# State-space scan on tiles of 32 channels by 4 states: factors in PSUM, both products on GpSimd

## The chip, the core and the metric

The kernel runs on one core of a Trainium2 chip. A core has five engines that run their own instruction streams in order and meet only through semaphores: TensorE (PE, matmuls), VectorE (DVE), ScalarE (ACT), GpSimd (POOL) and SyncE (SP), which here issues all DMAs. Data lies in SBUF (128 partitions), in PSUM (eight banks, into which PE writes; DVE and ACT reach it too), or in memory outside the core.

The metric is the time of one execution on the device in microseconds (us). Durations of single instructions are in nanoseconds (ns) where marked so.

## What is computed

Eight batches of 512 tokens with 256 channels pass through attention, an FFN whose operands are quantised to four bits, a Mamba block that works in both directions, and the FFN again. The change is in Mamba's scan. In one direction it reads, cut to what matters:

```python
def _ssm_dir(xs, conv_w, conv_b, xproj_w, dt_w, dt_b, A_log, D_skip):
    xc = jax.nn.silu(_causal_depthwise_conv(xs, conv_w, conv_b))
    x_dbl = xc @ xproj_w
    dt, B_ssm, C_ssm = jnp.split(x_dbl, [DT_RANK, DT_RANK + D_STATE], axis=-1)
    dt = jax.nn.softplus(dt @ dt_w + dt_b)
    A = -jnp.exp(A_log)
    dA = jnp.exp(dt[..., None] * A)
    dBu = dt[..., None] * B_ssm[:, :, None, :] * xc[..., None]
    def step(h, inp):
        dAt, dBut, ct = inp
        h = dAt * h + dBut
        y = jnp.einsum('bdn,bn->bd', h, ct)
        return (h, y)
    ...
    return y + xc * D_skip
```

There are 512 inner channels (d) and 16 states (n), so each batch and direction has 8192 recurrences over 512 tokens. For every one of them the kernel needs a decay factor exp(dt * A), a first product (dt * xc) * B, the recurrence, and a second product with C; the 16 states of a channel are then summed.

## The kernel before

**Streams.** The program is written as generators that are advanced in turns (`interleave`, `run`, L885 to L955): `thread_a` is attention of a batch, `thread_b` holds merge and second FFN of a finished batch, Mamba's front of the next and the first FFN of the one after, and `thread_s` is the scan. The loop at L953 runs the scan of batch b beside attention of b + 3 and the other work. A planner then orders the instructions of each engine before the run, with the scan at the lower priority (OS = 0 against OA = OB = 1000). The order that each engine gets is fixed in the program.

**Preparation of a scan.** `ssm_prep` (L773) does half of the channels (256) of one direction at a time: it computes dt (softplus written out: Relu, Abs, Exp and Ln on ACT, two sums on POOL at L811 and L813, two steps on DVE at L812 and L815), and u = dt * xc on POOL (L816). Both stay in SBUF with two channel blocks side by side, 128 partitions by 2 x 512. B and C of all states go to memory (bcd).

**Scan.** `ssm` (L819) has channels on the partitions. One round treats one state of 256 channels: SP loads B and C of that state, spread over all partitions (rep, L825); ACT writes the factors (abuf, L829; two instructions of 512, since A is a scalar of each partition); DVE makes the first product (L830) and the scan (L834) over both blocks at once, with an empty column between them where h starts again at zero; POOL makes the second product (L835); PE transposes the tiles onto one PSUM bank for each block, adding up the 16 states (L838). After 16 rounds ACT copies the sums (L844), PE turns them back (L848 through L127), and DVE adds xc * D (L852). There are 32 such passes of 16 rounds: 512 in all. All four operands of scan and products lie in SBUF; there is one factor buffer (NA = 1) and three of h (NH4 = 3).

**Other work that the text speaks of.** `roped` and `latents` (L374, L397) make attention's rotated latents: DVE multiplies out of PSUM (L384), POOL adds (L386) and takes the low parts (L403). `fp4` (L490) quantises: a product on POOL (L506), three steps on DVE (L507 to L509), a product on POOL (L510), with small DVE steps ahead of them (L498 to L503). `newton_rsqrt` (L267) is a chain of tiny DVE steps (L273 to L275). `conv` (L685) has DVE's L693 and L695 with all operands in SBUF; `mamba_pre` has L733. `mm` (L92) is the helper under whose line (L98) most matmuls stand. PSUM banks are named at L86: pa and po for attention, pb for FFN and merge, pp for Mamba's front and preparation, y0 and y1 for the scan's sums.

Of the kernel before, what the change touches and what calls it, by code (L numbers as in the profile page):

```python
# [35 lines left out]
def shape_constants():  # L36
    """Tables and masks that depend on shapes alone, side by side in one array."""
# [16 lines left out]
    parts = [("cos", cos), ("sin", sin), ("m8", mask8), ("m4", mask4), ("id", ident), ("up", up), ("lo", lo), ("rot", rot)]  # L54
# [8 lines left out]
def tile_hybrid(ctx: ExitStack, tc: tile.TileContext, w: dict, consts: bass.AP, out: bass.AP):  # L63
# [11 lines left out]
    PB, TB, HB, QB, QA, HT = 2, 3, 3, 3, 2, 1  # L75
    LAG, TC, XB, YT = 2, 4, 3, 2
    NH4, NA, NU, NDT, TA, RB = 3, 1, 3, 2, 2, 4
# [8 lines left out]
    BANKS = {"pa": 2, "po": 1, "pb": 2, "pp": 1, "y0": 1, "y1": 1}  # L86
# [13 lines left out]
    # ---------------------------------------------------------------- constants  # L100
# [11 lines left out]
    m8, m4, ident = cview("m8"), cview("m4"), cview("id")  # L112
# [16 lines left out]
    def split_rows(dst, row, n):  # L129
        """row [1, n] on partition 0 -> dst [2, n] float32r with the high and the low part."""  # L130
        hl = work([1, 2, 512], FPR, "rep", RB)
        S.copy(hl[:, 0, :n], row)
        V.tensor_tensor(hl[:, 1, :n], row, hl[:, 0, :n].bitcast(F32), ALU.subtract)
        nc.sync.dma_start(dst[0:1, :n].bitcast(F32), hl[:, 0, :n].bitcast(F32))
        nc.sync.dma_start(dst[1:2, :n].bitcast(F32), hl[:, 1, :n].bitcast(F32))

    # ------------------------------------------------------- attention weights
# [15 lines left out]
    def prep_attention():  # L153
        caw = []
        for k in range(3):
            caw.append(work([P, 2, C], F32, "u", NU))
            nc.sync.dma_start(caw[k], w["c_attn_w"][2 * k * P : (2 * k + 2) * P, :].rearrange("(a p) c -> p a c", p=P))
# [84 lines left out]
        # cproj, transposed, and the vector that every bias behind the softmax adds up to  # L242
# [23 lines left out]
    # ------------------------------------------------------------- layer norm  # L266
    def newton_rsqrt(dst, v, n, th):  # L267
        """dst = v ** -0.5 by Newton's iteration; v becomes -v / 2."""
# [8 lines left out]
    def stats(src, th, twice=False):  # L277
        """Means of the rows of src [P, NT, C] and the reciprocal square roots of variance + eps; with twice, behind
        these what two layer norms in a row scale by: the second acts on variance / (variance + eps)."""
# [28 lines left out]
    def token_transpose(dst, src, tag="pb"):  # L308
        """src [P, NT, C] tokens on partitions -> dst [P, 2, T] channels on partitions."""
# [6 lines left out]
    # -------------------------------------------------------------- attention  # L316
    def attention_front(b):
        """The normalised rows, transposed, and the latents of the first four heads."""
# [55 lines left out]
    def roped(xT, g, q):  # L374
        """Rotated latents of four heads [latent, token]; q: 0 for queries, 1 for keys."""
# [13 lines left out]
    def spill(hl, order):  # L389
        """hl [(head, latent), high/low, token] -> memory [part, latent, head, token] with the parts in order."""  # L390
# [6 lines left out]
    def latents(xT, g):  # L397
        """High and low parts of the keys and of the queries of four heads, in memory."""
# [18 lines left out]
    # (head of a pair, number of tiles before the last one) whose scores share a bank  # L417
    PACKS = [[(0, 3)], [(1, 3)], [(0, 2), (0, 0)], [(1, 2), (1, 0)], [(0, 1), (1, 1)]]

    def heads(g, lat, y):  # L420
        qst = [work([98, 2, T], FPR, f"qst{pr}", 1) for pr in range(2)]
        for pr in range(2):
# [3 lines left out]
            # row maxima, negated  # L426
# [62 lines left out]
    # -------------------------------------------------------------------- FFN  # L489
    def fp4(dst, src, n, tag, twice=False, pp=P):  # L490
        """Block-wise FP4 quantise and dequantise of src [pp, n] along the free dim into dst. A multiple of the step
        (half of the power of two below the value, at least 0.5) is what is left when 1.5 * 2**23 steps have been added
        and taken away again; or-ing 22 << 23 into an exponent of 128 or 129 adds 22 to it, and leaves a smaller one
        below 149."""
# [53 lines left out]
    def ffn_front(src):  # L548
        """The normalised and quantised rows, transposed."""
# [52 lines left out]
    def ffns(jobs):  # L602
        """One FFN after the other, as one stream of row tiles; the rows of the next are made ready meanwhile."""
# [26 lines left out]
    # ------------------------------------------------------------------ Mamba  # L630
# [4 lines left out]
    Aneg = const([P, 2, ND, NS], F32, "Aneg")  # L635
# [4 lines left out]
    abuf = [const([P, 2, T + 1], F32, f"abuf{i}") for i in range(NA)]  # L640
    hbuf = [const([P, 2, T + 1], F32, f"hbuf{i}") for i in range(NH4)]
    for t in abuf + hbuf:
        G.memset(t, 0.0)
# [6 lines left out]
    def prep_mamba():  # L650
# [4 lines left out]
        win = [work([P, 2 * INNER], F32, "dt", NDT) for _ in range(2)]  # L655
# [15 lines left out]
        for d, sx in enumerate(("", "_b")):  # L671
            wxp = work([P, 2, T], F32, "tmpA", TA).rearrange("p a t -> p (a t)")[:, : ND * 96].rearrange("p (m n) -> p m n", m=ND)
# [4 lines left out]
            nc.sync.dma_start(Aneg[:, d], w["A_log" + sx].rearrange("(a p) n -> p a n", p=P))  # L677
# [19 lines left out]
    def mamba_pre(src, scr):  # L697
# [13 lines left out]
        token_transpose(xT, xn, "pp")  # L711
        yield
        for m in range(8):
            wp = work([P, 2, P], F32, "xrf", XB)
            nc.sync.dma_start(wp, win_d[m])
            o = psum("pp")
# [56 lines left out]
    def ssm_prep(b, d, c, scr):  # L773
        """Step sizes of half the channels in one direction and their products with the input; B and C in memory."""
        sx = ("", "_b")[d]
        if c == 0:
            us = []
            for i in range(2):
                us.append(work([P, 2, T], F32, "u", NU))
                nc.sync.dma_start(us[i], scr["xc"][4 * d + 2 * i : 4 * d + 2 * i + 2].rearrange("m p t -> p m t"))  # L780
            wxp = work([P, 2, T], F32, "tmpA", TA).rearrange("p a t -> p (a t)")[:, : ND * 96].rearrange("p (m n) -> p m n", m=ND)
            nc.sync.dma_start(wxp, wxp_d[d])
            o = psum("pp")
            for m in range(ND):
                mm(o[:96, :], wxp[:, m, :], us[m // 2][:, m % 2, :], start=(m == 0), stop=(m == ND - 1))
# [4 lines left out]
            fronts[(b, d)] = us, bcd  # L790
            yield
        us, bcd = fronts[(b, d)]
        u = us[c]
        wdt = work([DTR + 1, 2 * P], F32, "wdt", 1)
        cs = slice(2 * c * P, (2 * c + 2) * P)
        nc.sync.dma_start(wdt[:DTR, :], w["dt_w" + sx][:, cs])
        nc.sync.dma_start(wdt[DTR : DTR + 1, :], w["dt_b" + sx][cs].rearrange("(o n) -> o n", o=1))
        dt = work([P, 2, T], F32, "dt", NDT)
        prep[(b, d, c)] = dt, u, bcd
        ex = work([P, 2, T], F32, "tmpA", TA)  # L800
        for e in range(2):
            o = psum("pp")
            PE.matmul(o, wdt[:, e * P : (e + 1) * P], dbt[: DTR + 1, :], start=True, stop=True)
            S.activation(dt[:, e, :], o, AF.Relu)
            S.activation(ex[:, e, :], o, AF.Abs)
            yield
        S.activation(ex, ex, AF.Exp, scale=-1.0)
        lg = work([P, 2, T], F32, "tmpA", TA)
# [7 lines left out]
        G.tensor_tensor(u, dt, u, ALU.mult)  # L816
        yield

    def ssm(b, d, scr):  # L819
        for c in range(2):  # L820
            dt, u, bcd = prep.pop((b, d, c))
            yps = [psum(f"y{i}") for i in range(2)]
            for n in range(NS):
                bcr = work([P, 2, T], F32, "rep", RB)
                nc.sync.dma_start(bcr, bcd[n][None].to_broadcast([P, 2, T]))  # L825
                seq[0] += 1
                a, h = abuf[seq[0] % NA], hbuf[seq[0] % NH4]
                for m in range(2):
                    S.activation(a[:, m, 1:], dt[:, m, :], AF.Exp, scale=Aneg[:, d, 2 * c + m, n : n + 1])  # L829
                V.tensor_tensor(h[:, :, 1:], u, bcr[:, 0, None, :].to_broadcast([P, 2, T]), ALU.mult)  # L830
                aflat, hflat = a.rearrange("p m t -> p (m t)"), h.rearrange("p m t -> p (m t)")
                if d == 1:
                    aflat, hflat = aflat[:, ::-1], hflat[:, ::-1]
                V.tensor_tensor_scan(hflat, aflat, hflat, 0.0, ALU.mult, ALU.add)  # L834
                G.tensor_tensor(h[:, :, 1:], h[:, :, 1:], bcr[:, 1, None, :].to_broadcast([P, 2, T]), ALU.mult)  # L835
                for m in range(2):
                    for i in range(NT):
                        PE.matmul(yps[m][:, i * P : (i + 1) * P], h[:, m, 1 + i * P : 1 + (i + 1) * P], ident,  # L838
                                  start=(n == 0 and i == 0), stop=(n == NS - 1 and i == NT - 1), is_transpose=True)
                yield  # L840
            yts = []
            for i in range(2):
                yts.append(work([P, T], F32, "yt", YT))
                S.copy(yts[i], yps[i])  # L844
            for i in range(2):
                o = psum("pp")
                for q in range(NT):
                    transpose(o[:, q * P : (q + 1) * P], yts[i][:, q * P : (q + 1) * P])  # L848
                xp = work([P, T], F32, "xp", 1)
                m = 2 * c + i  # L850
# [53 lines left out]
    def preps():  # L904
        for b in range(B):
            for d in range(2):
                for c in range(2):
                    yield lambda b=b, d=d, c=c: ssm_prep(b, d, c, scrs[b])
# [79 lines left out]
```

## Time and profile before

| | value |
|---|---|
| time, median of 3 runs | 4627.51 us (4624.49 to 4628.98) |
| the profiled execution: its span from first to last instruction | 4625.4 us |
| PE busy | 3244.4 us, 70% of the span, 12904 matmuls |
| DVE busy | 4028.7 us, 87% |
| ACT busy | 1592.1 us, 34% |
| POOL busy | 2201.7 us, 48% |
| DMA | 628.44 MB, 41.9% of the time of 16 DMA engines |
| TensorE clock granted, mean | 0.804 |

The profile gives the span alone; the median of the runs is 2.1 us above it.

A row of a group reads: line, engine, operation, tile written <- tiles read, shapes, count | busy us in total, mean ns of one | idle us of the engine just before, and what ended most of that. A row of one line's spread has minimum, median and maximum of the duration in ns after the count, then first and last start. A row of the timeline has start and duration in us, and in brackets the idle time before it and what ended it. A row of the windows gives, for a stretch of the span, busy us of PE, weight loads, DVE, ACT and POOL with instruction counts, then the granted clock, the DMA share and GB/s. An instruction that has been issued and cannot proceed counts as busy: its row gets longer.

### The profile page before, as it was taken

What the parts mean: (1) busy time and instruction counts of PE and PEld (TensorE: products, weight loads), DVE (VectorE), ACT (ScalarE), POOL (GpSimd) and SP (SyncE); (2) the same over time, 40 slices, a digit from 0 to 9 for tenths busy, and PEclk for the clock granted to TensorE, in tenths of its full rate; (3) what the DMA queues carried; (4) which work ended last, traced back from release to release, by engine and by line L of the source; (5) the groups of instructions that cost most, each with busy time, mean ns of one, the idle gap of its engine ahead of it and who ended that gap; (6) DMA issues with size and microseconds to landing.
All of it is one profiled execution on the core that took longest, in us unless ns stands there. A gap on an engine that the chain in (4) does not pass through costs nothing. (4 is left out here: it accounts for less than half of the span.)

```text
span 4625.4 us, 40263 instructions
## 1 busy us (share of the span) xinstructions
PE 3244.4 (70%) x12904; PEld 2000.0 (43%) x12904; DVE 4028.7 (87%) x4087; ACT 1592.1 (34%) x2725; POOL 2201.7 (48%) x929
## 2 busy tenths in 40 slices
PE   4879777787776678777777777768745566466456
PEld 2334344344444345444544444445533344345344
DVE  5235599897999996999989998999999999999983
ACT  1223432543443333333343333433433324332320
POOL 3011365445445653545444564565455554555551
PEclk8779878888887799888888888878866777677678
DMA  5223433444454344543454344533543244425232
GB/s 138 85 82 103 141 133 115 152 145 147 159 188 138 115 130 156 166 148 121 153 180 156 119 139 159 185 114 119 167 140 125 100 130 162 147 100 189 98 103 88
DMA packets 349922, 628.44 MB, mean 136 GB/s; under 512 B 50029, under 2 KB 195726, under 8 KB 349710
## 3 DMA queue, kind: packets, MB, share of 16 engines
q1 hardware_dynamic: 349710, 625.85, 41.9%
q8 instruction: 103, 1.69, 0.2%
q14 instruction: 109, 0.89, 0.1%
HBM read 506.85 MB, written 118.88 MB: 135 GB/s over the span
## 5 line engine op out<-in xcount | busy, mean ns | idle before, releaser
L835 POOL TENSOR_TENSOR hbuf<-hbuf,rep 128x1024 f32<-128x1024 f32 x512 | 1304.8, 2549 | 1505.4 <-DVE hbuf L834 688.3
L834 DVE TENSOR_TENSOR_SCAN hbuf<-abuf,hbuf 128x1026 f32<-128x1026 f32 x512 | 1357.7, 2652 | 32.8 <-ACT abuf L829 30.7
L829 ACT ACTIVATE abuf<-dt,Aneg 128x512 f32<-128x512 f32 x1024 | 684.9, 716 | 1699.9 <-DVE hbuf L834 1688.0
L830 DVE TENSOR_TENSOR hbuf<-u,rep 128x1024 f32<-128x1024 f32 x512 | 911.6, 1786 | 37.0 <-issue 19.6
L838 PE MATMUL y<-cst,hbuf 128*128 128x128 f32 x4096 | 690.5, 322 | 355.2 <-POOL hbuf L835 346.7
L838 PEld LDWEIGHTS y<-cst,hbuf 128*128 128x128 f32 x4096 | 579.1, 169 | 517.8 <-POOL hbuf L835 422.9
L98 PE MATMUL pb<-wgu,fxT 128*128 128x352 f32 x1024 | 427.9, 555 | 167.8 <-DVE hff L573 55.5
L433 PE MATMUL pa<-kst,qst 96*128 96x512 f32 (+3 forms) x512 | 229.9, 497 | 237.3 <-DVE tmp L384 100.9
L474 PE MATMUL po<-pt,vs 128*32 128x512 f32 (+3 forms) x1024 | 343.5, 481 | 4.3 <-ACT pt L469 4.2
L98 PEld LDWEIGHTS pb<-wgu,fxT 128*128 128x128 f32 x1024 | 211.5, 223 | 311.3 <-DVE hff L573 75.8
L98 PE MATMUL pa<-xT,wp 128*128 128x512 f32 x512 | 288.1, 694 | 50.4 <-DVE mx L443 29.3
L386 POOL TENSOR_TENSOR tmp<-tmp,tmp 128x512 f32<-128x512 f32 x64 | 124.4, 1944 | 405.8 <-DVE tmp L384 247.6
L98 PE MATMUL pb<-qv,hff 128*128 128x256 f32 x1024 | 261.4, 402 | 38.5 <-DMA qv<-sy 36.0
L98 PE MATMUL pb<-wdn,hT 128*128 128x256 f32 (+1 forms) x768 | 238.9, 455 | 34.5 <-ACT hT L588 14.6
L469 ACT ACTIVATE pt<-pa 128x512 f32<-128x512 f32 x320 | 186.0, 591 | 197.4 <-PE pa L466 135.5
L433 PEld LDWEIGHTS pa<-kst,qst 96*128 96x128 f32 x512 | 120.0, 235 | 305.3 <-DVE tmp L384 123.6
L443 DVE TENSOR_REDUCE mx<-pa 128x1 f32<-128x512 f32 (+2 forms) x384 | 179.0, 497 | 82.7 <-PE pa L435 82.4
L693 DVE SCALAR_TENSOR_TENSOR tmpB<-xs,cw,tmpB 128x512 f32<-128x512 f32 x192 | 243.0, 1265 | 7.6 <-ACT tmpB L691 6.1
L464 PE MATMUL pa<-qst,kst 98*128 98x512 f32 (+3 forms) x512 | 213.5, 464 | 50.4 <-ACT pt L469 23.3
L98 PEld LDWEIGHTS pb<-qv,hff 128*128 128x128 f32 x1024 | 197.3, 201 | 86.0 <-DMA hff<-in_merge_w 22.9
L98 PEld LDWEIGHTS pb<-wdn,hT 128*128 128x128 f32 (+1 forms) x768 | 161.1, 225 | 93.2 <-issue 25.8
L510 POOL TENSOR_TENSOR hff<-qv,qns 128x704 f32<-128x704 f32 x66 | 143.7, 2177 | 104.7 <-DVE qv L509 79.0
(207 smaller groups left out, 4899.3 us busy)
## 6 DMA issues: line engine op xcount, KB each, us to landing
rep<-bcd SPq DMA_DIRECT2D x512, 512.0 KB
hld<-hl SPq DMA_DIRECT2D x192, 256.0 KB
hff<-in_merge_w SPq DMA_DIRECT2D x128, 256.0 KB
qv<-sy SPq DMA_DIRECT2D x128, 256.0 KB
kst<-hld SPq DMA_DIRECT2D x64, 384.0 KB
qst<-hld SPq DMA_DIRECT2D x64, 384.0 KB
wp<-wqk_d SPq DMA_DIRECT2D x64, 256.0 KB
sxc<-tmpB SPq DMA_DIRECT2D x64, 256.0 KB
```

Of the source, the lines that this page charges most:

```text
L98: PE.matmul(o, L, R, start=start, stop=stop, **kw)
L433: PE.matmul(o[:, at : at + n], qst[pr][:96, j, i * P : (i + 1) * P], kst[:96, j, :n], start=(k == 0), stop=False)
L443: V.tensor_reduce(M[:, j, i : i + 1], o[:, at : at + n], AX.X, ALU.max, negate=True)
L464: PE.matmul(o[:, at : at + n], kst[:, j, kt * P : (kt + 1) * P], qst[pr][:, j, kt * P :], start=(k == 0), stop=False)
L469: S.activation(pt, o, AF.Exp)
L474: PE.matmul(po[c : c + 32, kt * P :], vs[:, kt, h * VW : h * VW + 32], pt[:, at : at + n], start=(kt == 0), stop=(kt == 2), tile_position= ...
L693: V.scalar_tensor_tensor(acc, tap(k), cw[:, d, m, k : k + 1], acc, ALU.mult, ALU.add)
L829: S.activation(a[:, m, 1:], dt[:, m, :], AF.Exp, scale=Aneg[:, d, 2 * c + m, n : n + 1])
L830: V.tensor_tensor(h[:, :, 1:], u, bcr[:, 0, None, :].to_broadcast([P, 2, T]), ALU.mult)
L834: V.tensor_tensor_scan(hflat, aflat, hflat, 0.0, ALU.mult, ALU.add)
L835: G.tensor_tensor(h[:, :, 1:], h[:, :, 1:], bcr[:, 1, None, :].to_broadcast([P, 2, T]), ALU.mult)
L838: PE.matmul(yps[m][:, i * P : (i + 1) * P], h[:, m, 1 + i * P : 1 + (i + 1) * P], ident, start=(n == 0 and i == 0), stop=(n == NS - 1 and ...
```

## The change

Channels and states share the partitions: a tile holds 32 channels (q counts four such blocks of 128) times 4 states (g counts four such groups), over 512 tokens. dt and u of a block of 128 channels now go to memory (dud) and come back, each of the four q with its 32 rows repeated for four states; B and C of four states are loaded once for a direction and kept. The factors go to PSUM banks (a), the first product moves from DVE to POOL, and the scan and the second product take a tile of 512. The four tiles of a group are summed over states by four matmuls with a 0/1 matrix (sel, 128 x 32), each into its own 32 columns of PE and its own 32 partitions of one PSUM bank (y); the first of them is made to wait for the group's last product. Transposes, their copies on ACT and the turning back are gone.

```diff
-    PB, TB, HB, QB, QA, HT = 2, 3, 3, 3, 2, 1
-    LAG, TC, XB, YT = 2, 4, 3, 2
-    NH4, NA, NU, NDT, TA, RB = 3, 1, 3, 2, 2, 4
+    PB, TB, HB, QB, QA, HT = 2, 3, 3, 2, 1, 1
+    LAG, TC, XB = 2, 3, 3
+    NHB, NDU, NU, NDT, TA, RB = 8, 5, 4, 2, 3, 5
...
-    BANKS = {"pa": 2, "po": 1, "pb": 2, "pp": 1, "y0": 1, "y1": 1}
+    BANKS = {"pa": 2, "po": 1, "pb": 2, "a": 2, "y": 1}
...
+    sel = (p[:, None] % 32 == np.arange(32)[None, :]).astype(np.float32)
...
-    def ssm_prep(b, d, c, scr):
+    def ssm_prep(b, d, m, scr):
...
         V.tensor_tensor(dt, dt, ex, ALU.add)
         G.tensor_tensor(u, dt, u, ALU.mult)
+        dud = dr.tile([P, 2, T], F32, tag="dud", name=f"dud_{b}_{d}_{m}", bufs=8)
+        prep[(b, d, m)] = dud, fronts[(b, d)]
+        nc.sync.dma_start(dud[:, 0, :], dt)
+        nc.sync.dma_start(dud[:, 1, :], u)
         yield
...
     def ssm(b, d, scr):
-        for c in range(2):
-            dt, u, bcd = prep.pop((b, d, c))
-            yps = [psum(f"y{i}") for i in range(2)]
-            for n in range(NS):
-                bcr = work([P, 2, T], F32, "rep", RB)
-                nc.sync.dma_start(bcr, bcd[n][None].to_broadcast([P, 2, T]))
-                seq[0] += 1
-                a, h = abuf[seq[0] % NA], hbuf[seq[0] % NH4]
-                for m in range(2):
-                    S.activation(a[:, m, 1:], dt[:, m, :], AF.Exp, scale=Aneg[:, d, 2 * c + m, n : n + 1])
-                V.tensor_tensor(h[:, :, 1:], u, bcr[:, 0, None, :].to_broadcast([P, 2, T]), ALU.mult)
...
-                V.tensor_tensor_scan(hflat, aflat, hflat, 0.0, ALU.mult, ALU.add)
-                G.tensor_tensor(h[:, :, 1:], h[:, :, 1:], bcr[:, 1, None, :].to_broadcast([P, 2, T]), ALU.mult)
-                for m in range(2):
-                    for i in range(NT):
-                        PE.matmul(yps[m][:, i * P : (i + 1) * P], h[:, m, 1 + i * P : 1 + (i + 1) * P], ident,
-                                  start=(n == 0 and i == 0), stop=(n == NS - 1 and i == NT - 1), is_transpose=True)
...
+        bcs = None
+        for m in range(ND):
+            dud, bcd = prep.pop((b, d, m))
+            if bcs is None:
+                bcs = []
+                for g in range(4):
+                    bc = work([P, 2, T], F32, "rep", RB)
+                    src = bcd.rearrange("(j g) k t -> g j k t", g=4)[g]
+                    nc.sync.dma_start(bc, src[:, None].to_broadcast([4, 32, 2, T]))
+                    bcs.append(bc)
+            dus = []
+            for q in range(4):
+                du = work([P, 2, T], F32, "du", NDU)
+                nc.sync.dma_start(du, dud[32 * q : 32 * q + 32][None].to_broadcast([4, 32, 2, T]))
+                dus.append(du)
...
+            y = psum("y")
+            for g in range(4):
+                bc, hs = bcs[g], []
+                for q in range(4):
+                    a = psum("a")
+                    S.activation(a, dus[q][:, 0, :], AF.Exp, scale=Aneg[:, d, 4 * m + q, g : g + 1])
+                    h = work([P, T], F32, "h", NHB)
+                    G.tensor_tensor(h, dus[q][:, 1, :], bc[:, 0, :], ALU.mult)
+                    if d == 0:
+                        V.tensor_tensor_scan(h, a, h, 0.0, ALU.mult, ALU.add)
+                    else:
+                        V.tensor_tensor_scan(h[:, ::-1], a[:, ::-1], h[:, ::-1], 0.0, ALU.mult, ALU.add)
+                    last = G.tensor_tensor(h, h, bc[:, 1, :], ALU.mult)
+                    hs.append(h)
...
+                for q in range(4):
+                    i = PE.matmul(y[32 * q : 32 * q + 32, :], sel, hs[q], start=(g == 0), stop=(g == 3), tile_position=(0, 32 * q))
+                    if q == 0:
+                        tc.add_manual_dep(i.ins, last.ins.name, mybir.DependencyInfo(mybir.DependencyClass.Sync, mybir.DependencyReason.DATA),
+                                          reason="the four sums side by side")
...
+            V.scalar_tensor_tensor(xp, xp, Dh[:, d, m : m + 1], y, ALU.mult, ALU.add)
+            nc.sync.dma_start(scr["y"][4 * d + m], xp)
```

`preps` and `thread_s` follow: preparation goes by blocks of 128 channels (m), four of them ahead of the first scan where there were two, and a round of `thread_s` is half of a group g. Mamba's front and preparation take their PSUM banks from pb, since pp is gone. Aneg is laid out for the new tiles.

## Prediction

> **What bounds the kernel now.** The first part of the page says VectorE (DVE), 87% of the span. The windows say where, and the costliest groups on what:
>
> ```profile
> 0.00:545.00 545.00, 410.79 (x1421) 205.66 (x1421) 241.17 (x555) 147.18 (x282) 94.46 (x76) 0.82 0.37 109
> 545.00:4508.00 3963.00, 2756.12 (x11189) 1740.09 (x11187) 3744.55 (x3439) 1433.07 (x2415) 2091.52 (x842) 0.80 0.43 141
> 4508.00:4626.00 118.00, 77.49 (x296) 54.27 (x296) 43.02 (x93) 11.84 (x28) 15.77 (x13) 0.83 0.26 86
> L834 DVE TENSOR_TENSOR_SCAN hbuf<-abuf,hbuf 128x1026 f32<-128x1026 f32 x512 | 1357.7, 2652 | 32.8 <-ACT abuf L829 30.7
> L830 DVE TENSOR_TENSOR hbuf<-u,rep 128x1024 f32<-128x1024 f32 x512 | 911.6, 1786 | 37.0 <-issue 19.6
> L835 POOL TENSOR_TENSOR hbuf<-hbuf,rep 128x1024 f32<-128x1024 f32 x512 | 1304.8, 2549 | 1505.4 <-DVE hbuf L834 688.3
> ```
>
> The windows' columns after the length are PE, weight loads, DVE, ACT, POOL. I cut the span at the first and last product of L835: 545 us of start-up, 3963 us of scanning (DVE busy 94%), 118 us of tail. Only the middle matters. But is DVE working there, or waiting? The spread of each line's durations (minimum/median/maximum, ns) and a piece of the timeline answer:
>
> ```profile
> L384 DVE SCALAR_TENSOR_TENSOR tmp<-pa,bcol,cst x128: 645/739/752, 53.8 to 3104.8; 128x512 f32<-128x512 f32 x128
> L693 DVE SCALAR_TENSOR_TENSOR tmpB<-xs,cw,tmpB x192: 657/747/2843, 432.5 to 3928.3; 128x512 f32<-128x512 f32 x192
> L834 DVE TENSOR_TENSOR_SCAN hbuf<-abuf,hbuf x512: 2224/2283/4449, 541.1 to 4502.8; 128x1026 f32<-128x1026 f32 x171
> L830 DVE TENSOR_TENSOR hbuf<-u,rep x512: 1154/1220/3378, 537.7 to 4493.5; 128x1024 f32<-128x1024 f32 x171
> L386 POOL TENSOR_TENSOR tmp<-tmp,tmp x64: 1260/1706/3517, 55.3 to 3106.0; 128x512 f32<-128x512 f32 x64
> 2204.07 2.18 POOL L835 TENSOR_TENSOR hbuf<-hbuf,rep 128x1024 f32<-128x1024 f32 x1 [3.03 <-DVE hbuf L834]
> 2204.27 1.99 DVE L274 TENSOR_TENSOR nrq<-nrq,lnve 128x4 f32<-128x4 f32 x1
> ...
> 2221.18 2.18 POOL L835 TENSOR_TENSOR hbuf<-hbuf,rep 128x1024 f32<-128x1024 f32 x1 [2.36 <-PE y L838]
> 2221.62 2.83 DVE L830 TENSOR_TENSOR hbuf<-u,rep 128x1024 f32<-128x1024 f32 x1
> ...
> 2230.64 1.19 DVE L830 TENSOR_TENSOR hbuf<-u,rep 128x1024 f32<-128x1024 f32 x1
> 2230.84 3.05 POOL L835 TENSOR_TENSOR hbuf<-hbuf,rep 128x1024 f32<-128x1024 f32 x1 [3.77 <-DVE hbuf L834]
> ```
>
> L274 handles four elements in 1.99 us: it ends at 2206.26, and L835 at 2206.25. At 2221.62 L830 takes 2.83 instead of 1.19, again until POOL is done. At 2230.84 it is POOL that waits. So a DVE instruction with both inputs in SBUF and a POOL product exclude each other. The first two rows show the exception: the same operation at the same size, up to 2843 ns with inputs in SBUF (L693), never above 752 with one input in PSUM (L384). **The bound is what the two engines share**; I call it the port.
>
> I add up the port's load at undisturbed durations, less what neighbouring records overlap (0.04 us on POOL, 0.07 on DVE, read off back-to-back rows):
> - second products, POOL: 512 x (2.18 - 0.04) = 1096
> - other POOL work: rows L386, L403, L506, L510, L811, L813, L816 at their shortest, about 603, of which some 100 outside the scan phase: 502
> - scans: 512 x (2.26 - 0.07) = 1121; first products, L830: 512 x (1.18 - 0.07) = 568
> - other DVE instructions that show such stretching (L273 to L275, L500, L503, L507 to L509, L693, L695, L733, L812, L815): 546 at their shortest, 453 less overlaps, about 394 in the phase
>
> Sum 3681 of 3963: the port is 92.9% used.
>
> **The change part by part.**
>
> *Scan.* The factors now lie in PSUM (tile a), so the scan has one SBUF input and, by the L384/L693 pair, leaves the port: -1121. On DVE it still costs 1024 x 2.28 x 512/1026 = 1165 (estimate), where 512 took 1358. No row has a scan with a PSUM operand. At best it stays out of the port; at worst it holds it as now, +1024 x 1.08 = 1106. I take the first: L384, L852, L412 and L755 all have one operand in PSUM, and none stretches.
>
> *First product to POOL, second product in half-size tiles.* 2048 products 128x512, nearest row L386, shortest 1.26: 2048 x (1.26 - 0.04) = 2499, for 568 + 1096 now. Half-size tiles lose: two of 1.26 replace one of 2.18. [...] By rows and lock the change costs 2499 - 568 - 1096 - 1121 = -286.
>
> *Preparation* in 64 pieces of 128 channels for 32 of 256: the three POOL sums take 192 x 1.22 = 234 for 96 x 2.31 = 222; DVE's two some 4 more. +16 on the port.
>
> New load: 3681 - 286 + 16 = 3411, POOL's own share 502 + 12 + 2499 = 3013.
>
> *DVE.* 3745 less 1358 (L834) and 912 (L830) leaves 1475 with its waits, plus 1165: 2640, some 71% of the new phase. The remaining waits stay alike: POOL would hold the port 81% of the time with ops of 1.26 (mean rest 0.51), now 40% with 2.18 (0.44). DVE is covered by POOL.
>
> *ACT.* Still 1024 exponentials of 0.714; no row writes one to PSUM. Bounds: L588's 0.58 to 0.9, i.e. -137 to +190, on an engine 36% busy in the phase; I take 0.71. 64 copies (L844, 36 us) go; up to 64 more table loads of 1.28 (82 us) come. The single factor buffer, for whose release ACT waited 1688 us, becomes two banks. All hidden behind POOL; nothing counted.
>
> *PE.* 4096 transposing matmuls (690 us) and 256 transposes (51) go; 1024 matmuls of 512 columns come: at the 0.69 of the 128x512 row of L98 711 us one after another, a quarter side by side. So -31 to -564 on an engine at 70%: hidden. The first of four now waits for the fourth product, with FFN and attention matmuls queued behind it; but the next products that need these tiles' buffers stand at least 4 POOL instructions (4.9 us) later in the built order.
>
> *DMA and SP.* 512 broadcast loads become 64 plus 256 of the same 512 KB; 128 stores of dud are added, and 32 loads of u at 512 KB become 128 at half: 628 MB falls to about 580. SP's rows go from 2081 to 2175. A load of du waits for a buffer of the block before; in a place of the built order that I read, eleven POOL instructions (13 us) lie between that release and the product that needs the load. Behind it on SP wait attention's and the FFN's loads. POOL's work hides this, and no longer does if a load takes more than those 13 us.
>
> *Smaller pools* (QB, QA, TC one less; bank pp merged into pb) tighten FFN and Mamba's front. In the start-up, which POOL doesn't cover, I bound it with the round trip of dud at 0 to 30 us and take 5. The tail stays 118.
>
> **Sum.** One in-order engine now carries 3013 of the 3411, so I take 92% use, a little under before: 3411/0.92 = 3707. With 550 and 118: **4375 us**, against a span of 4625.4; the median of the three runs, 4627.5, is 2 above the span, so it stands for both.
>
> **Rivals.**
> 1. *POOL's queue stalls.* Break-even is where the phase is 3959 again: 86% use. In the built order the second product stands mostly seven or more POOL instructions behind the last POOL result that DVE needs to reach its scan; in 150 of 1024 cases at most three. If each of those exposes a scan and one DVE instruction (1.1 + 0.9), 300 us come on top: **4675**, slower. From 250 us, 1.7 each, it decides. For: when DVE and POOL both lag, the queues lock step. Against: 874 have cover, and DVE is only 71% busy.
> 2. *The PSUM scan still takes the port*: (3411 + 1106)/0.929 + 668 = **5530**, slower. Against: four rows without exception.
> 3. *The port fills as in the best window*: from 3000 to 3500 DVE is busy 493 of 500. 3411/0.98 + 668 = **4150**.
> 4. *The period is set by other chains*: attention, both FFNs and merge pass through PE, ACT and two pb banks, and POOL's order holds their products. Then the phase stays: **4625**. For: PE 70%; against: it leaves work, and DVE sheds 30%.
>
> **How the numbers follow.** Forecast 0.57 (own range 4280 to 4520, from 94.5 to 88.5% use), rival 1 0.22, rival 2 0.05, rival 3 0.10, rival 4 0.06. The range 4200 to 4740 leaves out rival 2 and the ends of 1 and 3, under 0.2. A difference within 0.2% (9 us) can't be told from none. Faster: 0.57 + 0.10 + a third of rival 4 = 0.69; same 0.03; slower 0.28.
>
> **What would show it.** Scan rows of 1.1 to 1.2 us that never stretch; products at 1.26 with the port free; POOL busy over 90% of the phase, DVE near 70%; POOL's gaps naming scans in tens of us. Wrong: POOL under 85% with gaps that name DVE or PE (rival 1 or 4), scans with maxima of 2.4 (rival 2), or products with a median well over 1.4.

## The result and the profile after

The changed kernel takes 5192.91 us (median of 4 runs, 5182.99 to 5197.06), the kernel before beside it 4628.24 us: a ratio of 1.1216, 95% interval 1.1200 to 1.1232. It is slower by 565 us, outside the predicted range. The profiled execution's span is 5181.2 us.

From the page of the changed kernel, the busy times and the groups that stand where L830 and L835 stood:

```profile
PE 2992.7 (58%) x10600; PEld 1487.8 (29%) x10600; DVE 2970.3 (57%) x4151; ACT 1675.5 (32%) x2789; POOL 3344.2 (65%) x2557
q1 hardware_dynamic: 352174, 575.53, 34.3%
L845 POOL TENSOR_TENSOR h<-du,rep 128x512 f32<-128x512 f32 x1024 | 1342.4, 1340 | 711.1 <-PE y L855 556.8
L850 POOL TENSOR_TENSOR h<-h,rep 128x512 f32<-128x512 f32 x1024 | 1356.4, 1350 | 216.7 <-DVE h L847 114.1
```

Its scan phase as one window (columns as before the change: length, busy time of PE, PEld, DVE, ACT and POOL, granted clock, DMA share, GB/s):

```profile
560.00:5060.00 4500.00, 2499.60 (x8948) 1229.16 (x8952) 2691.42 (x3510) 1528.22 (x2497) 3242.66 (x2471) 0.73 0.35 114
```

The scan, which stood in L834, now has a line for each direction. The rows by line, with the shortest, median and longest duration in ns, first and last start, and form:

```profile
L847 DVE TENSOR_TENSOR_SCAN h<-a,h x512: 1153/1210/1225, 587.1 to 4880.3; 128x512 f32<-128x512 f32 x171
L849 DVE TENSOR_TENSOR_SCAN h<-a,h x512: 1153/1212/1225, 908.4 to 5051.3; 128x512 f32<-128x512 f32 x171
...
L845 POOL TENSOR_TENSOR h<-du,rep x1024: 1250/1267/2088, 585.8 to 5050.0; 128x512 f32<-128x512 f32 x171
```

Read these first for what went as forecast. No scan takes more than 1225 ns: with the factors in PSUM none of the 1024 is stretched, so they have left the port. Products take 1267 ns in the median, for 1260 assumed. DVE's busy time fell by a quarter. And yet the scan phase grew from 3963 to 4500 us, with no engine busy more than 72% of it (POOL: 3243 of 4500). The time is in waits. The waits view names who ended them (us in total, times, longest). A selection, with POOL's longest first; ACT's waits for scans are longer still, but ACT is busy only a third of the span:

```profile
POOL h L845 <- PE y L855: 556.8, 110, 20.3
ACT a L843 <- DMA du<-dud: 292.5, 64, 12.7
PE pb L99 <- DMA qv<-sy: 275.7, 33, 30.0
DVE lnstf L284 <- DMA fxn<-sx: 115.7, 16, 33.6
PE pa L465 <- DMA qst<-md: 88.4, 14, 13.5
```

The first row looks like the culprit: POOL waits for PE to sum up and so free the h buffers. But PE itself waits for DMAs of other streams: qv<-sy belongs to the merge, qst<-md to attention. Before the change those two rows were small:

```profile
PE pb L98 <- DMA qv<-sy: 36.0, 19, 9.3
PE pa L464 <- DMA qst<-md: 10.0, 5, 3.5
```

One stall in the timeline shows how they hang together:

```profile
1497.12 0.31 SPq L454 DMA_DIRECT2D md<-yT  x1
1497.54 6.93 SPq L834 DMA_DIRECT2D du<-dud  x2
1512.52 0.23 SPq L455 DMA_DIRECT2D qst<-md  x1
...
1523.90 0.77 PE L465 MATMUL pa<-qst,kst 98*128 98x512 f32 x1 [12.27 <-DMA qst<-md]
...
1524.73 1.94 PE L855 MATMUL y<-h,cst 128*32 128x512 f32 x8
...
1526.73 4.94 POOL L845 TENSOR_TENSOR h<-du,rep 128x512 f32<-128x512 f32 x4 [20.34 <-PE y L855]
```

Attention's maxima take a round trip through memory, 8 KB each way (md). Between the two DMAs SP has issued two more loads of du. From the first DMA to PE's matmul the trip takes 27 us; PE waits for it with L465, the sums L855 stand behind L465 in PE's queue, and POOL behind the sums. Why do 8 KB take so long? Three windows, the last two inside that stall:

```profile
1482.00:1512.00 30.00, 17.69 (x57) 7.67 (x49) 17.21 (x21) 8.68 (x15) 24.39 (x19) 0.56 0.26 94
1502.00:1512.00 10.00, 4.41 (x18) 2.12 (x17) 0.00 (x0) 1.98 (x4) 4.39 (x4) 0.50 0.26 103
1518.00:1523.00 5.00, 0.00 (x0) 0.00 (x0) 0.00 (x0) 0.00 (x0) 0.00 (x0) 0.50 0.26 105
```

From 1518 to 1523 every engine stands still, and DMA runs at a share of 0.26 and 105 GB/s. 0.26 of sixteen engines is about four. A load of du or of B and C is written with four repeats of 32 rows, and 512 KB at 103 GB/s take 5.1 us. By this estimate 320 such loads take 1630 us at a share of a quarter. Nor do two of them get two quarters: SP had issued four loads of du, two from 1491.41 and two from 1497.54 to 1504.47, and after that the share stays at 0.26 until 1512. At 103 GB/s these 7.5 us move about 770 KB, more than one load, so at least two narrow transfers were outstanding, and together they had the share of 0.26.

### The profile page after: what moved, and what is told of

Read it like the earlier page. It is cut to its first block, busy times and chain, and to the rows that moved or that the text cites. A ratio compares the mean times of both kernels' runs of the same rounds, so it can differ in the third digit from the quotient of the medians.

```text
span 5181.2 us, 38511 instructions
## 1 busy us (share of the span) xinstructions
PE 2992.7 (58%) x10600; PEld 1487.8 (29%) x10600; DVE 2970.3 (57%) x4151; ACT 1675.5 (32%) x2789; POOL 3344.2 (65%) x2557
## 3 DMA queue, kind: packets, MB, share of 16 engines
q1 hardware_dynamic: 352174, 575.53, 34.3%
## 5 line engine op out<-in xcount | busy, mean ns | idle before, releaser
L845 POOL TENSOR_TENSOR h<-du,rep 128x512 f32<-128x512 f32 x1024 | 1342.4, 1340 | 711.1 <-PE y L855 556.8
L850 POOL TENSOR_TENSOR h<-h,rep 128x512 f32<-128x512 f32 x1024 | 1356.4, 1350 | 216.7 <-DVE h L847 114.1
L843 ACT ACTIVATE a<-du,Aneg 128x512 f32<-128x512 f32 x1024 | 704.3, 690 | 1549.0 <-DVE h L847 634.5
L849 DVE TENSOR_TENSOR_SCAN h<-a,h 128x512 f32<-128x512 f32 x512 | 610.2, 1210 | 245.0 <-POOL h L845 192.6
L847 DVE TENSOR_TENSOR_SCAN h<-a,h 128x512 f32<-128x512 f32 x512 | 609.7, 1208 | 127.9 <-POOL h L845 101.4
L855 PE MATMUL y<-h,cst 128*32 128x512 f32 x2048 | 367.5, 780 | 465.1 <-POOL h L850 465.1
L99 PE MATMUL pb<-qv,hff 128*128 128x256 f32 x1024 | 306.9, 458 | 378.0 <-DMA qv<-sy 275.7
L99 PEld LDWEIGHTS pb<-qv,hff 128*128 128x128 f32 x1024 | 230.6, 232 | 474.4 <-DMA qv<-sy 240.0
L387 POOL TENSOR_TENSOR tmp<-tmp,tmp 128x512 f32<-128x512 f32 x64 | 84.0, 1313 | 404.9 <-DVE tmp L385 263.2
L465 PE MATMUL pa<-qst,kst 98*128 98x512 f32 (+3 forms) x512 | 223.6, 485 | 149.0 <-DMA qst<-md 88.4
L692 DVE SCALAR_TENSOR_TENSOR tmpB<-xs,cw,tmpB 128x512 f32<-128x512 f32 x192 | 195.5, 1018 | 109.7 <-ACT tmpB L690 108.2
L855 PEld LDWEIGHTS y<-h,cst 128*32 128x32 f32 x2048 | 48.7, 122 | 638.3 <-POOL h L850 551.3
```

The lines of the kernel that those rows point to most:

```text
L99: PE.matmul(o, L, R, start=start, stop=stop, **kw)
L465: PE.matmul(o[:, at : at + n], kst[:, j, kt * P : (kt + 1) * P], qst[pr][:, j, kt * P :], start=(k == 0), stop=False)
L692: V.scalar_tensor_tensor(acc, tap(k), cw[:, d, m, k : k + 1], acc, ALU.mult, ALU.add)
L843: S.activation(a, dus[q][:, 0, :], AF.Exp, scale=Aneg[:, d, 4 * m + q, g : g + 1])
L845: G.tensor_tensor(h, dus[q][:, 1, :], bc[:, 0, :], ALU.mult)
L847: V.tensor_tensor_scan(h, a, h, 0.0, ALU.mult, ALU.add)
```

## The experiments

Each was timed beside the kernel before on the same chip; times are medians, ratios are to that kernel. The planner makes a new order for every kernel, and the order alone can move the time: in e18, the one run that turns it, by 1.3% (61 us). Smaller steps between two variants can't be ascribed to their edit.

### First round: the queues, the engine, the pools

**e1**: without the manual wait.

```diff
-                    if q == 0:
-                        tc.add_manual_dep(i.ins, last.ins.name, ...)
```

> The changed kernel without the wait that holds the first of four sums until the group's last product. Theory Q (queues: POOL waits for h buffers, which only PE's in-order queue sets free, where the sums stand behind other matmuls): the wait adds to that, so a gain, 4950 to 5130 us, and POOL's 557 us of waiting for PE shrink by a third or more. Theory S (smaller pools and the merged PSUM banks make the other streams late): 5160 to 5220 us. Theory C (POOL's own load, one in-order engine): 5160 to 5220 us.

5197.47 us, 1.1215 (1.1183 to 1.1248). No gain: the wait costs nothing. POOL's waiting for PE falls only from 557 to 449 us. What the wait is for does happen: the same 2048 records of the sums keep PE busy 1019 us without it and 367.5 with it (the first row is e1, the second the changed kernel).

```profile
L855 PE MATMUL y<-h,cst 128*32 128x512 f32 x2048 | 1019.0, 720 | 422.1 <-POOL h L850 333.2
L855 PE MATMUL y<-h,cst 128*32 128x512 f32 x2048 | 367.5, 780 | 465.1 <-POOL h L850 465.1
```

**e2**: sums only for the last group.

```diff
-                for q in range(4):
+                for q in range(4 if g == 3 else 0):
...
-                    i = PE.matmul(..., start=(g == 0), stop=(g == 3), tile_position=(0, 32 * q))
+                    i = PE.matmul(..., start=True, stop=True, tile_position=(0, 32 * q))
```

> The changed kernel with the sums over states of only the last of the four groups; the sums of the other three are left out (the output lacks them), and their h buffers come free with POOL's second product. POOL's and DVE's work is the same. Theory Q: POOL's 557 us of waiting for PE fall below 200 us and the time to 4600 to 4850 us. Theory S: 5050 to 5200 us, since the other streams keep their pools. Theory C: 5100 to 5200 us, since POOL keeps every product.

5203.86 us, 1.1229 (1.1196 to 1.1261). With three quarters of the sums gone, POOL's waiting for PE falls from 557 to 127 us, and the time doesn't move (4 us above the bands of S and C). The wait was handed on, to the loads of du; in the changed kernel the first of these rows read 142.8 us:

```profile
POOL h L845 <- DMA du<-dud: 580.7, 159, 19.1
POOL h L845 <- PE y L855: 126.8, 24, 15.0
```

Theory Q falls for the loss as a whole.

**e3**: the first product on DVE.

```diff
-                    G.tensor_tensor(h, dus[q][:, 1, :], bc[:, 0, :], ALU.mult)
+                    V.tensor_tensor(h, dus[q][:, 1, :], bc[:, 0, :], ALU.mult)
```

> The changed kernel with the first product back on DVE (128x512, about 0.66 us each, both inputs in SBUF), scan from PSUM and second product on POOL as changed. The port's load falls by 1024 x (1.22 - 0.60) = 635 us to about 2780 us, POOL's own by 1249 us. Theory C: 4300 to 4600 us. Theory Q: it is now DVE that waits for h buffers; 4850 to 5150 us. Theory S: 4950 to 5150 us.

5256.14 us, 1.1342 (1.1309 to 1.1375), above every band. 1249 us less work for POOL bring nothing; now it is DVE that waits for du, 632 us. Theory C falls too, as long as the fault of the loads is in.

**e4**: the kernel before, with the smaller pools.

```diff
-    PB, TB, HB, QB, QA, HT = 2, 3, 3, 3, 2, 1
-    LAG, TC, XB, YT = 2, 4, 3, 2
+    PB, TB, HB, QB, QA, HT = 2, 3, 3, 2, 1, 1
+    LAG, TC, XB, YT = 2, 3, 3, 2
...
-            o = psum("pp")
+            o = psum()
```

> The kernel before with the smaller pools alone: QB 3 to 2, QA 2 to 1, TC 4 to 3, and Mamba's front and preparation on the pb banks instead of pp. The scan stays as it was. Theory S: 4850 us or more, most of the change's loss. Theories Q and C: 4610 to 4700 us.

4900.57 us, 1.0574 (1.0535 to 1.0614): 265 us, nearly half of the change's loss, from buffers alone. So theory S has a part, in that kernel. But PE's waits for DMAs, qv<-sy at 56.1 us and qst<-md at 9.1, stay near what they were before. None of the three explains the whole, and the share of 0.26 in the trace led to a fourth, D. Its four of 16 DMA engines are an estimate from that share (16 x 0.26 = 4.2); no view names the engines that work off a transfer.

### Second round: the form of the loads

**e5**: the changed kernel, each load as four DMAs of 32 partitions.

```diff
-                    nc.sync.dma_start(bc, src[:, None].to_broadcast([4, 32, 2, T]))
+                    for j in range(4):
+                        nc.sync.dma_start(bc[32 * j : 32 * j + 32], src[j][None].to_broadcast([32, 2, T]))
...
-                nc.sync.dma_start(du, dud[32 * q : 32 * q + 32][None].to_broadcast([4, 32, 2, T]))
+                for j in range(4):
+                    nc.sync.dma_start(du[32 * j : 32 * j + 32], dud[32 * q : 32 * q + 32])
```

> The changed kernel with every load of du and of B and C (destination 128 partitions, written as 4 x 32 rows) issued as four DMAs of 32 partitions; bytes and data are the same. Theory D (a transfer whose pattern begins with 4 is worked off by 4 of the 16 DMA engines: 102 GB/s and a DMA share of 0.26 in the slices that these loads fill, so 320 x 5.1 us, with everything behind them on those engines): share in such slices above 0.5, time 4650 to 4950 us. Theory S (smaller pools alone): 5100 to 5220 us. Theory R (the round trip of dt and u through memory, whatever the width): 5100 to 5220 us.

4630.73 us, 0.9997 (0.9987 to 1.0008): 562 us come back, 19 more than theory D's band allowed. From its page:

```profile
PE 2941.8 (64%) x10600; PEld 1472.3 (32%) x10600; DVE 3014.5 (65%) x4151; ACT 1677.6 (36%) x2789; POOL 3345.2 (72%) x2557
q1 hardware_dynamic: 371374, 575.61, 43.8%
```

The row that pointed at PE, and PE's two rows for DMAs:

```profile
POOL h L847 <- PE y L857: 223.3, 74, 14.8
PE pb L99 <- DMA qv<-sy: 116.2, 37, 7.1
PE pa L465 <- DMA qst<-md: 14.4, 5, 4.9
```

The same 575 MB in 560 us less; the queue's share of sixteen engines' span goes from 34.3% to 43.8%. Where 16 DMAs of du, four whole loads, follow each other, the window from 2013 to 2024 has a share of 0.61 and 196 GB/s, above the 0.5 that theory D asked for. POOL's waiting for PE shrinks from 557 to 223 us, though nothing was done to PE.

**e6**: the converse, the kernel before with its load in the other form.

```diff
-                nc.sync.dma_start(bcr, bcd[n][None].to_broadcast([P, 2, T]))
+                nc.sync.dma_start(bcr, bcd[n][None, None].to_broadcast([4, 32, 2, T]))
```

> The kernel before with nothing changed but the form of its load of B and C: 4 x 32 repeated rows where it was 128; bytes and data are the same. Theory D: each of the 512 loads takes about 5.1 us instead of some 2.5, 2600 us of four engines' time; 4850 to 5300 us. Theories S and R: 4620 to 4680 us.

5186.78 us, 1.1197 (1.1154 to 1.1239). The form of one load, with the same bytes, costs the old kernel 555 us. In it even DVE waits for the load, and the other streams for theirs, as in the changed kernel:

```profile
DVE hbuf L830 <- DMA rep<-bcd: 285.6, 97, 10.2
PE pb L98 <- DMA qv<-sy: 179.6, 39, 14.3
PE pa L464 <- DMA qst<-md: 58.7, 18, 10.0
```

This kernel has the old pools, so the smaller ones aren't what makes those two rows long. e5 and e6 together settle the loss: it is the form of the loads, as in theory D.

**e7**: e5 and e3 together.

> Loads in four as in the run beside it, and the first product on DVE. If DMA is what held the changed kernel, engines matter again: the port's load is some 2780 us against 3411, and the time 50 to 250 us below that of loads in four alone. Theories S and R: no better than it, within 50 us.

4482.51 us, 0.9677 (0.9644 to 0.9709), 148 us below e5: once DMAs flow, work taken off POOL and the port counts.

**e8**: the kernel before, with only the factors moved to PSUM.

```diff
-                for m in range(2):
-                    S.activation(a[:, m, 1:], dt[:, m, :], AF.Exp, scale=...)
...
-                V.tensor_tensor_scan(hflat, aflat, hflat, 0.0, ALU.mult, ALU.add)
+                for m in range(2):
+                    a, hm = psum("a"), h[:, m, 1:]
+                    S.activation(a, dt[:, m, :], AF.Exp, scale=...)
...
+                    V.tensor_tensor_scan(hm, a, hm, 0.0, ALU.mult, ALU.add)
```

> The kernel before with the factors in one PSUM bank (two scans of 512 instead of one of 1026), for which Mamba's front and preparation move to the pb banks; products, loads and pools as before. The scans leave the port (-1121 of 3681 us). If the port bounds the kernel before: 4250 to 4550 us. If it doesn't, or if one bank makes ACT and DVE alternate, or if pb is the narrow place: 4650 to 4950 us.

4372.14 us, 0.9438 (0.9402 to 0.9475). 259 us less: this part of the change is a gain when it stands alone, as it should be if the port bounds the kernel before. One bank is enough for it. Its scans of one direction (the other's longest is 1225 ns):

```profile
L834 DVE TENSOR_TENSOR_SCAN hbuf<-a,hbuf x512: 1150/1211/1228, 518.8 to 4066.9; 128x512 f32<-128x512 f32 x171
```

Splitting the scan is not by itself the gain: two of 1.21 us are longer than the undisturbed one of 2.28. Whether the finer steps help ACT, DVE and POOL to overlap was not tried alone. The whole 1121 us do not come back; DVE looks like the next bound, busy 3363 of 3705 us in the window from 545 to 4250, rows stretched by the port included.

### Third round: why e5 is at 4631 and not at 4375, and what is best

The names are numbers of buffers: QB and QA for the quantiser's tiles qv and qa (qv also takes the merge's loads), TC for tmpB, NDU for du, RB for rep, NHB and NH4 for h in the changed and in the old kernel.

**e9**: e5 with QB 3, QA 2, TC 4, paid for with NDU 4 and RB 4.

> The changed kernel with loads in four and the pools of before (QB 3, QA 2, TC 4); the room comes from one buffer less each for du (5 to 4) and for B and C (5 to 4). After loads in four the time was that of before, 4631 us, with POOL busy 72%. If the smaller pools hold the rest of the gain back (they cost the kernel before 265 us): 4380 to 4530 us. If POOL's queue itself does: 4600 to 4680 us. If the fifth buffer of du carries the change from one channel block to the next: 4680 us or more.

4596.2 us, 0.9924 (0.9904 to 0.9944): 35 us below e5, just outside the bands given and within what the order alone can do. Small pools are no large part of what is left, unless the missing du buffer hides a gain.

**e10**: the kernel before with QB, QA and TC one less, and pp kept.

> The kernel before with QB, QA and TC one less, Mamba's front and preparation on their own bank pp as before. With both cuts it took 4901 us. If the SBUF buffers make that: 4850 to 4910 us. If the PSUM bank does: 4630 to 4680 us. The kernel with factors in PSUM had no pp either and took 4372 us, which speaks for the SBUF buffers.

4709.39 us, 1.0169 (1.0148 to 1.0189): between the bands. 76 of e4's 265 us come with the SBUF buffers alone; the other 189 need the merged bank as well. The merged bank alone was not run in the old kernel; e8 lacks pp too and is fast, but its factors are in PSUM.

**e11**: e7 with the old pools and NHB 4.

> Loads in four, first product on DVE, the pools of before, and four h buffers instead of eight to make room. It was 4482 us with the small pools. If small pools cost as much here as in the kernel before: 4220 to 4340 us. If four h buffers tie POOL and DVE together: 4450 us or more.

4702.94 us, 1.0155 (1.0135 to 1.0175), 220 us above e7: four h buffers are too few, and tie the engines together. Five to seven were not tried.

**e12**: e8, with attention's stores (`spill`) also in four.

```diff
-            nc.sync.dma_start(d[r].rearrange("l h t -> h l t"), hl[:, k, :].bitcast(F32))
+            for j in range(4):
+                nc.sync.dma_start(d[r][:, j, :], hl[LAT * j : LAT * (j + 1), k, :].bitcast(F32))
```

> The kernel before with factors in PSUM, and attention's stores of its latents (256 KB, 4 x 32 rows) issued as four DMAs each. They are the other transfers that show a DMA share of 0.27. Theory D: they leave the path of attention sooner; 4250 to 4370 us. If nothing waits for them, or SP's 576 more issues cost as much: 4370 to 4450 us.

4281.08 us, 0.9245 (0.9230 to 0.9261). The old kernel had narrow transfers of its own, worth 91 us here. Its trace showed them: just after three of these stores, issued from 1043.73 to 1046.58, a window of the kernel before reads

```profile
1047.00:1050.00 3.00, 2.02 (x6) 1.71 (x7) 3.00 (x6) 2.55 (x5) 2.45 (x2) 0.77 0.26 95
```

**e13**: e5 with the sums of e2.

> Loads in four, and the sums over states of only the last of the four groups; the other three groups' sums are left out. Without loads in four this changed nothing (5204 us). Loads in four alone took 4631 us, with 223 us in which POOL waited for PE to free an h buffer. Theory Q, on what is left: those waits go, and the time falls to 4350 to 4500 us. If PE's queue only hands on other waits (DVE, DMA, the planner's order): 4560 to 4640 us.

4649.35 us, 1.0037 (1.0024 to 1.0050): no gain, 9 us above the higher band. PE's queue isn't what holds e5 either.

**e14**: e5 with bank pp back and one bank for the factors.

> Loads in four, and Mamba's front and preparation on a bank of their own again (pp), for which the factors have one bank instead of two. If the merged banks hold the rest back: 4400 to 4560 us. If POOL's queue does: 4600 to 4680 us. If one factor bank makes ACT, DVE and POOL alternate: 4680 us or more; in the kernel before with PSUM factors one bank did not prevent 4372 us.

4676.57 us, 1.0099 (1.0076 to 1.0122): in the band of POOL's queue, 46 us above e5. So there is no sign that the merged banks hold e5 back; a loss from the second factor bank, which had to go, could hide a small gain.

**e15**: e5 with e12's stores.

> Loads in four, and attention's stores of its latents in four as well, which took 91 us off the kernel before with PSUM factors. If narrow DMAs still hold the changed kernel: 4480 to 4570 us. If not: 4600 to 4660 us.

4552.91 us, 0.9832 (0.9812 to 0.9851): 78 us, as expected of narrow DMAs.

**e16**: e12 with NH4 = 4.

> The kernel before with PSUM factors and stores in four, and a fourth h buffer in the room that the factors left in SBUF. It was 4281 us. If DVE and POOL still wait for each other's buffers: 4180 to 4260 us. If the port and DVE (84% busy) bound it: 4265 to 4300 us.

4253.60 us, 0.9186 (0.9167 to 0.9204), within the lower band, though its 27 us over e12 are less than what the order can do. It is the fastest kernel of the study that computes everything, 377 us faster than the kernel before by three small edits. Its engines:

```profile
PE 3152.5 (74%) x12904; PEld 1964.9 (46%) x12904; DVE 3638.2 (86%) x4599; ACT 1612.8 (38%) x2725; POOL 1973.9 (46%) x929
```

**e17**: e5 without the second product, so that the states are summed without C.

> Loads in four, and POOL's second product left out (the states go into the sums without C), and with it the wait of the first sum for it. POOL loses 1024 x 1.22 = 1249 us, the port as much. If POOL or the port holds the 4631 us of loads in four: 3700 to 4150 us, until DVE or PE is the next. If the other streams (attention, FFN, merge) and their planned order do: 4400 to 4600 us.

4063.87 us, 0.8781 (0.8727 to 0.8836): 567 us for 1249 us of POOL's work, in the band of "POOL or the port"; the edit takes the work off both, so it can't tell one from the other. The next bound is not far below: in this kernel POOL's first products wait mostly for du.

```profile
L847 POOL TENSOR_TENSOR h<-du,rep 128x512 f32<-128x512 f32 x1024 | 1348.4, 1345 | 805.0 <-DMA du<-dud 421.1 <-PE y L857 283.3 <-DMA xc<-sxc 15.5
```

**e18**: e15 with the planner's priorities turned.

```diff
-    OA, OB, OS = 1000, 1000, 0
+    OA, OB, OS = 0, 0, 1000
```

> Loads and stores in four as in e15 (4553 us), with the planner's priorities turned: scan 1000, attention and the other streams 0. If the planned order is what leaves POOL idle 28% of the time, it moves by more than 2% either way: 4300 to 4460 us if the scan was held back by the others, 4650 us or more if the others are the longer chain. If the order doesn't matter: 4510 to 4600 us.

4491.64 us, 0.9706 (0.9657 to 0.9754): 61 us below e15, between the bands. This turn of the order moves the time by 1.3%, not by the 250 us in question.

## Why the prediction was wrong

**The step that failed** is the one on DMA and SP. It counted loads, bytes and SP rows, found less traffic than before, and took a load of du as good as a load of rep because both have 512 KB; then it let POOL's 13 us of work hide it. It never asked what form the new pattern had. By the estimate above one load takes 5.1 us and the four of a channel block 20, together at a share of 0.26, and not only scans but the other streams' round trips wait longer: PE's waits for qv<-sy are 275.7 us, for 36.0 before and 116.2 in e5. The condition named in the prediction, that POOL's work no longer hides a load of more than 13 us, was met by the four together. I put this at 0; e5 and e6 give 562 and 555 us. The diff showed the other form: `to_broadcast([4, 32, 2, T])` against `to_broadcast([P, 2, T])`. The trace of before had a warning as well: attention's stores have 4 x 32 rows too, three of them are followed by a share of 0.26 at 95 GB/s, and e12 and e15 show their price of 91 and 78 us. A slip without weight: the traces have 2167 and 2269 DMAs issued by SP, before and after, where I had counted 2081 and 2175.

**The bound before**: right as far as tested. The sum of 3681 of 3963 us was not measured as such, but factors in PSUM alone bring 259 us (e8).

**Scan**: right that it leaves the port (maximum 1225 ns); 1.21 us each for 1.14 forecast. No run shows the lock that the sum of -286 us names beside the rows; they show durations: 2283 ns in the median and up to 4449 with the factors in SBUF, for 1026 columns, and 1210 to 1212, never above 1225, with the factors in PSUM, for 512.

**Products on POOL**: right at 1.27 us. But for the first product POOL was the wrong engine. By the rows of before 1024 elements take 1.19 us on DVE (L830) and 2.52 in two halves on POOL (L386, 1.26 at its shortest), and without the fault of the loads the kernel is 148 us faster with that product on DVE (e7 against e5). Whether that comes from room in POOL's queue or on the port, no run separates.

**Use of the port**: too high. From e5's windows, its scan phase:

```profile
567.00:4502.00 3935.00, 2446.78 (x8909) 1210.65 (x8908) 2734.44 (x3507) 1523.35 (x2485) 3243.67 (x2471) 0.76 0.45 129
```

In 3935 us the load of 3411 us makes 86.7%, not 92%. 3411/0.867 - 3411/0.92 = 227 us of the 256 by which e5 misses the sum; most of the rest is start-up, 567 for 550 us. e17 points to POOL or the port, e13 speaks against the sums' queue and e14 against the merged banks, narrow stores are 78 us (e15), pools and order some 35 and 61 (e9, e18). A single wait that makes up the difference was not found; why the use stays at 86.7% is open.

**Smaller pools**: mis-sized in kind. I costed them in the start-up at 5 us; in the old kernel they cost 265 us (e4), and not there: its second products start at 541 us, as before, and the last of them starts 255 us later. In e5 they cost at most some 35 (e9).

**PE and the manual wait**: right that they are hidden (e1, e2, e13). With the wait the sums keep PE busy for 0.36 of the time without it (367.5 of 1019.0 us, e1), where a quarter was taken as the best case. ACT's exponentials take 0.69 us for 0.71 assumed; no run tests whether ACT is hidden.

**Rivals**: rival 1 named an unusable rest of the port and 4675 us. With the loads mended its sign came true, POOL busy 82% of the phase with gaps that name DVE and PE, at its break-even of 86%. But the cost that it counted is only half there: the gaps before POOL's second product that name scans sum to 144 us in e5, for 300. The result itself, 5193 us, came from none of the four.

## What to carry over

Compare the form of a moved or new DMA with the one whose duration is taken for it: bytes and count are not enough. Here 4 x 32 rows for 128, with both the same, cost 555 us (e6). A plateau of the DMA share at 0.26, while engines stand still, was its mark. When POOL's longest wait is for an engine that is itself half idle, follow that engine's own waits before believing it, and test it by taking the work away: e2 cleared PE in one run, and the next row named the loads. And test the parts of a compound change singly: one of them, factors in PSUM, was worth 259 us while the whole lost 565.

## What the runs showed that I had not expected

A transfer of 4 x 32 rows moves about 103 GB/s at a DMA share of 0.26, and giving the old kernel's one load that form makes it 12% slower (e6). The four sums of a group, each in its own 32 columns, do run side by side when they are released together: their 2048 records keep PE busy 367.5 us with the manual wait and 1019 us without it, though one record is no shorter (780 and 720 ns in the mean), and the time is the same (e1). The granted clock was, in the main, lower where PE was busy for less of the span: 0.724 at 55% (e2), 0.739 at 58% (changed kernel), 0.791 at 67% (e1), 0.804 at 70% (before), 0.874 at 79% (e17). Why was not tested.
